# A two-layer graph network on one core: the first pass's weight product, from seven products of halves to fifteen products of thirds

## The chip, the cores and the metric

The kernel runs on one core of one Trainium2 chip. The metric is the device time of one launch in microseconds. Three runs before the change gave 2593.05, 2593.22 and 2594.38 us, a median of 2593.22 us. The profiled execution spans 2591.5 us, and all times of day below count from its start. The engines are named as in the profile: PE is the tensor engine's matmul stream, PEld its weight loads, DVE the vector engine, ACT the scalar engine, POOL GpSimd, SP the engine that issues the DMAs.

## The reference, cut to what matters

The input is x, 128 graphs of 64 nodes with 768 features, and an integer adjacency per graph. Two layers follow each other, each on the normalised and rectified x. The first one is where the change is:

```
h   = relu(layernorm(x))
ctx = adj @ (h @ Wadj.T) / deg + adj.T @ (h @ Wrev.T) / rdeg + h @ Wself.T + biases
x   = x + ctx + (relation counts) @ (embedding tables)
```

Since `adj @ (h @ W) = (adj @ h) @ W`, the kernel mixes the nodes first and multiplies by the weights afterwards. For every pair of 128-row tiles (four graphs, 256 rows), the three terms of ctx together are one product: 256 rows by (3 matrices x 768) inner elements by 768 columns, all in float32. The relation terms are small bfloat16 products of counts with a table, added to the same sums. The second layer is a graph attention with six heads and a gate; its two weight products are of the same kind with two matrices.

## The kernel before

**Two passes.** 8192 rows are 64 tiles of 128 rows, worked on as 32 pairs. The first pass does layer one for all pairs and writes h and x+h of layer two to DRAM; the second pass reads them back and does layer two. Each pass is a loop over pairs.

**The weight product in halves.** In `main(p)` of the first pass the product is taken as a 2x2x2 product of blocks: rows in two tiles, inner elements in two halves of 384, columns in two halves of 384. It is done with seven block products in place of eight (the Winograd form of Strassen's method). The left sums S1 to S4 are formed per pair: S1 and S3 by DVE straight from PSUM in `operands` (lines 441 and 442), S2 and S4 by POOL in `sum2` and `sum4` (lines 447 and 452). The right sums T1 to T4 are formed once, by DVE, at the start (line 184). A block product is 3 blocks of 128 inner elements times 3 matrices, 9 matmuls of 128x128 weights (line 466, the stationary side is the mixed h) against 128x384 moving elements. Every float32 matmul appears twice in the records, with two weight loads. Four PSUM banks, `pwa` to `pwd`, hold chains of partial sums, and after each product DVE adds the bank to a part of x (line 483). A bank that is continued must have been read by DVE before the next product writes it.

**Side work.** While pair p is multiplied, pair p+1 is prepared: load of x and adjacency, normalisation (`norm`, `stats`), mixing with the nodes (`operands`: 24 matmuls of 64 rows and 192 columns, line 422, copied from PSUM by ACT), and relation counts (`count`, `digits`, `count_t`). `finish(p)` normalises the result of pair p for layer two and stores it; its POOL part is a power of one element per row (line 166) and the sum x+h (line 526).

**What sets the order.** `merged(main, side)` interleaves the steps of `main` with entries of a side list, each with the number of the main step it comes before. A scheduler then orders every engine's queue within what dependences allow, apart from instructions marked `keep_in_program_order`. [...] Tiles come from pools with a fixed number of buffers; where a tile has no free buffer, its first writer waits for the last reader of an old one.

**Memory between the passes.** Blocks of weights lie in tiles of their own. The last pair of the first pass fetches the second pass's weights in `fetch` as blocks come free, and forms its T sums. x and the second pass's h share a ring of eight tiles (`bufs=8`, lines 194 and 236). The second pass's head sums `hs` and their swapped halves `hx` share a ring of seven.

Of the kernel before, what the change touches and what calls it, by code (L numbers as in the profile page):

```python
# [15 lines left out]
P = 128  # L16
EPS = 1e-5
NEG_MASK = -999.0
LEAKY = 0.2


@with_exitstack
def kernel(
# [47 lines left out]

    nc = tc.nc
# [11 lines left out]
    HALF = D // 2  # L84
    HH = H // 2
# [9 lines left out]
    assert GT == 2 and N == 64 and DO == P and H == KB and KB % 2 == 0 and H % 2 == 0  # L95
# [76 lines left out]
    def block(name, mats, place):  # L172
        return [keep.tile([P, KH, HALF], F32, name=f"{name}{s}", tag=f"w{place}{s}") if s < 2 else
                keep.tile([P, KH, HALF], F32, name=f"{name}{s}", tag="wl", bufs=7)
                for s in range(mats)]


    SUMS = {"T1": ("T3", "11"), "T2": ("22", "T1"), "T4": ("21", "T2"), "T3": ("22", "T3")}

    def sum_of_weights(w, to, behind=False):  # L180

        a, b = SUMS[to]
        for s, t in enumerate(w[to]):
            ins = nc.vector.tensor_sub(t, w[a][s], w[b][s])  # L184
            if behind:
                tc.keep_in_program_order(ins)


    bv, H1 = {}, {}

    def load_h(p):
        for k in range(2):
            t = 2 * p + k
            H1[t] = keep.tile([P, D], F32, name="h1", tag="x", bufs=8)
            nc.sync.dma_start(H1[t], H1D[p][k * P : (k + 1) * P, :])

    def fetch():

        def blk_of(name, place, h, q):
            bv[name] = block(f"bv{name}", 2, place)  # L200
            for s, src in enumerate((w_cat, hw_t)):
                nc.sync.dma_start(
                    bv[name][s],
                    src[h * HALF : (h + 1) * HALF, q * HALF : (q + 1) * HALF].rearrange(
                        "(k p) n -> p k n", p=P))

        def own(name, place):
            bv[name] = block(f"bv{name}", 2, place)

        return [(4, lambda: load_h(0)),  # L210
                (9, lambda: blk_of("11", "11", 0, 0)),
                (19, lambda: blk_of("21", "21", 1, 0)),
                (28, lambda: blk_of("T3", "T1", 0, 1)),
                (37, lambda: blk_of("22", "T2", 1, 1)),
                (47, lambda: (own("T1", "T4"), sum_of_weights(bv, "T1"), sum_of_weights(bv, "T3"))),
                (58, lambda: (own("T2", "T3"), sum_of_weights(bv, "T2")))]


    with ExitStack() as px:
# [7 lines left out]
        def load(p):  # L227
# [7 lines left out]
            for t in (2 * p, 2 * p + 1):  # L235
                X[t] = keep.tile([P, D], F32, name="x", bufs=8)
                nc.sync.dma_start(X[t], xf[t * P : (t + 1) * P, :])

        load(0)
# [3 lines left out]
        bia = work.tile([5, D], F32, name="bia", tag="s3")  # L243
        for i, v in enumerate((br, brr, badj, brev, bself)):
            nc.scalar.dma_start(bia[i : i + 1, :], row(v, 1))


        bw = {n: block(f"bw{n}", 3, n) for n in ("11", "21", "22", "T1", "T2", "T3", "T4")}

        def load_block(to, h, q):  # L250
            for s, src in enumerate((wadj_t, wrev_t, wself_t)):
                nc.sync.dma_start(
                    to[s], src.rearrange("(k h p) n -> h p k n", h=2, p=P)[h][:, :, q * HALF : (q + 1) * HALF])

        load_block(bw["11"], 0, 0)
        load(1)
        load_block(bw["21"], 1, 0)
        load_block(bw["T3"], 0, 1)
        load_block(bw["22"], 1, 1)
        wrt = work.tile([P, 2, D], F32, name="wrt", tag="a1")  # L260
        nc.sync.dma_start(wrt[:, 0, :], wr_t)
        nc.sync.dma_start(wrt[:, 1, :], wrr_t)
# [22 lines left out]
        def build_table():  # L285
# [21 lines left out]
            for hf in range(2):  # L307
                s = slice(hf * HALF, (hf + 1) * HALF)
                for d in range(2):
                    nc.tensor.matmul(pt[:NROW, hf, :HALF], es[:, d, :], wrt[:, d, s],  # L310
                                     start=(d == 0), stop=False)
                nc.tensor.matmul(pt[:NROW, hf, :HALF], eb, bia[:, s], start=False, stop=True)
            v = work.tile([P, D], F32, name="tv", tag="eq", bufs=1)
            qs = work.tile([P, 3, D], BF16, name="tq", tag="a22")
            nc.scalar.copy(v[:NROW].rearrange("p (a b) -> p a b", a=2), pt[:NROW, :, :HALF])
            for i in range(3):
                q = qs[:, i]
# [7 lines left out]
        A1, A22, S1, S2, S3, S4 = {}, {}, {}, {}, {}, {}  # L325
# [87 lines left out]
        def operands(p, k, q):  # L413
# [12 lines left out]
            pv = ps[:, :, : 6 * N].rearrange("p g (x n) -> p g x n", n=N)  # L426

            def blocks(ap):
                return ap.rearrange("p s (g n) -> p g s n", g=GT)

            if k == 0:
                if q == 0:
                    A1[p] = work.tile([P, KH, 2, 3, P], F32, name="a1")
                nc.scalar.copy(A1[p][:, q].rearrange("p h s (g n) -> p g (h s) n", g=GT), pv)  # L434
                return
            if q == 0:
                A22[p] = work.tile([P, KH, 3, P], F32, name="a22")
                S1[p] = work.tile([P, KH, 3, P], F32, name="s1", bufs=1)
                S3[p] = work.tile([P, KH, 3, P], F32, name="s3")
            nc.scalar.copy(blocks(A22[p][:, q]), pv[:, :, 3:])  # L440
            nc.vector.tensor_sub(blocks(S3[p][:, q]), blocks(A1[p][:, q, 0]), pv[:, :, :3])
            nc.vector.tensor_add(blocks(S1[p][:, q]), blocks(A22[p][:, q]), pv[:, :, :3])

        def sum2(p):
            S2[p] = work.tile([P, KH, 3, P], F32, name="s2", bufs=1)
            for q in range(KH):
                nc.gpsimd.tensor_sub(S2[p][:, q], S1[p][:, q], A1[p][:, q, 0])  # L447

        def sum4(p):
            S4[p] = work.tile([P, KH, 3, P], F32, name="s4", bufs=1)  # L450
            for q in range(KH):
                nc.gpsimd.tensor_sub(S4[p][:, q], A1[p][:, q, 1], S2[p][:, q])

        def main(p):

            bank = {}
            x0, x1 = X[2 * p], X[2 * p + 1]
            steps = []

            def mm(b, a, w, first):  # L460
                for q in range(KH):
                    for s in range(3):
                        def step(q=q, s=s):
                            if first and q == s == 0:
                                bank[b] = psw.tile([P, 512], F32, name=f"pw{b}")
                            nc.tensor.matmul(bank[b][:, :HALF], a()[:, q, s, :], bw[w][s][:, q, :],  # L466
                                             start=(first and q == s == 0),
                                             stop=(q == KH - 1 and s == 2),
                                             skip_group_check=True)
                        steps.append(step)  # L470

            def counts(b, k, q):
                def step():
                    for i, (a, e) in enumerate(PARTS):
                        nc.tensor.matmul(bank[b][:, :HALF], CT_T[p, k][: 3 * (e - a), i, :],  # L475
                                         tabs[i][:, q * HALF : (q + 1) * HALF],
                                         start=False, stop=True, skip_group_check=True)
                steps.append(step)

            def add(xt, q, b):  # L480
                def step():
                    v = xt[:, q * HALF : (q + 1) * HALF]
                    nc.vector.tensor_add(v, bank[b][:, :HALF], v)  # L483
                last = steps[-1]
                steps[-1] = lambda: (last(), step())

            mm("a", lambda: A1[p][:, :, 0], "11", True)
            add(x0, 0, "a")
            mm("c", lambda: A1[p][:, :, 1], "21", True)
            if p:  # L490
                counts("c", 0, 0)
                add(x0, 0, "c")
            mm("b", lambda: S1[p], "T1", True)
            add(x1, 1, "b")
            mm("a", lambda: S2[p], "T2", False)
            add(x0, 1, "a")
            mm("d", lambda: A22[p], "T4", True)
            if p:
                counts("d", 1, 0)
                add(x1, 0, "d")  # L500
            mm("a", lambda: S3[p], "T3", False)
            add(x1, 0, "a")
            mm("b", lambda: S4[p], "22", False)
            n = len(steps)
            counts("a", 1, 1)
            add(x1, 1, "a")
            if p:
                steps.insert(n - 4, steps.pop())
            else:
                counts("c", 0, 0)  # L510
                add(x0, 0, "c")
                counts("d", 1, 0)
                add(x1, 0, "d")
            counts("b", 0, 1)
            add(x0, 1, "b")
# [13 lines left out]
        def side(p):  # L529

            if p >= NP:
                return []
            return [(4, lambda: load(p + 1)),
# [3 lines left out]
                    (6, lambda: prep_r(p)),  # L537
                    (10, lambda: count(p, 0)),
                    (18, lambda: operands(p, 0, 0)),
# [424 lines left out]
```

## Time and profile before

| what | value |
|---|---|
| median time | 2593.22 us |
| PE busy / share of the span | 2543.7 us / 98% |
| weight loads (PEld) busy | 1525.5 us / 59% |
| DVE busy | 1765.7 us / 68% |
| ACT busy | 856.6 us / 33% |
| POOL busy | 733.4 us / 28% |
| one pair of the first pass, by the start of the same chain in neighbouring pairs | 47.36 us |
| first pass ends, first transpose of the second pass | 1554.2 us |
| granted PE clock | 0.994 of full speed |

A busy share is an average over the whole span. To judge a change in one stage, one looks at the period of that stage's loop and at what is idle or waits in it. Rows of the groups have the form: line, engine, operation, out<-in, shapes, count, then busy time in us, the mean of one in ns, and the idle time of the engine just before them with what ended it. Matmul records overlap in the pipeline, so the mean of one (490 ns) is longer than the distance from start to start.

### The profile page before, as it was taken

How to read it: one execution, taken by the hardware profiler on the slowest of the kernel's cores; microseconds unless marked ns; L12 is line 12 of the kernel's file. 1: busy time of each engine (PE TensorE's matmuls, PEld its weight loads, DVE VectorE, ACT ScalarE, POOL GpSimd, SP SyncE). 2: the span in 40 equal slices, each digit the busy share in tenths (PEclk: the TensorE clock that was granted, in tenths of full speed). 3: DMA queues.
4: the chain of work that ended last, by engine and by line, in shares of the span. 5: the costliest groups of instructions: out<-in, count | busy, mean ns of one | idle time of the engine just before them, and what ended most of it. 6: DMA issues, size and time to landing. Idle time of an engine off the chain costs nothing.

```text
span 2591.5 us, 31957 instructions
## 1 busy us (share of the span) xinstructions
PE 2543.7 (98%) x10924; PEld 1525.5 (59%) x10924; DVE 1765.7 (68%) x3887; ACT 856.6 (33%) x2596; POOL 733.4 (28%) x1055
## 2 busy tenths in 40 slices
PE   6999999999999999999999999999999999999996
PEld 3556666556566565565665655656566565565654
DVE  7856566565564665655655435888888888888888
ACT  1111112111111121111111104555555555555555
POOL 2331232232222312322223114333333333333332
PEclk9999999999999999999999999999999999999998
DMA  5112121121121111211211133333333333333322
GB/s 182 44 48 69 39 74 43 39 78 39 39 78 39 61 56 39 78 39 39 78 39 44 67 116 97 106 105 108 105 105 106 103 100 101 100 100 101 100 87 80
DMA packets 101572, 198.78 MB, mean 77 GB/s; under 512 B 35114, under 2 KB 43677, under 8 KB 101410
## 3 DMA queue, kind: packets, MB, share of 16 engines
q1 hardware_dynamic: 101256, 196.70, 23.9%
q8 instruction: 86, 1.41, 0.2%
q14 instruction: 76, 0.62, 0.1%
q10 hardware_dynamic: 154, 0.06, 0.0%
HBM read 95.67 MB, written 75.50 MB: 66 GB/s over the span
## 4 chain that ended last, share of the span: by engine, by line
PE 94%; DVE 3%; DMA 1%; ACT 1%; issue 1%; POOL 0%; SPq 0%; DVEq 0%; ACTq 0%; POOLq 0%
PE pwa L466 21%; PE pwb L466 14%; PE pma L675 14%; PE pmb L675 10%; PE pmc L675 9%; PE pwd L466 7%; PE pwc L466 7%; PE pb L422 5%; PE ps L835 2%; PE ps L646 2%; PE ps L819 1%; PE pwc L475 0%; DMA bw<-in_wadj_t_dram 0%; DVE bwT L184 0%; DMA x<-in_x_dram 0%
## 5 line engine op out<-in xcount | busy, mean ns | idle before, releaser
L466 PE MATMUL pwa<-bwT,s 128*128 128x384 f32 x1152 | 392.5, 490 | 0.4 <-DVE x L483 0.4
L466 PEld LDWEIGHTS pwa<-bwT,s 128*128 128x128 f32 x1152 | 215.5, 190 | 145.9 <-issue 8.0
L675 PE MATMUL pma<-bvT,s 128*128 128x384 f32 x768 | 279.4, 486 | 0.0
L447 POOL TENSOR_TENSOR s<-s,a 128x384 f32<-128x384 f32 x96 | 95.5, 1021 | 644.2 <-PE pwa L466 597.1
L483 DVE TENSOR_TENSOR x<-pwa,x 128x384 f32<-128x384 f32 x128 | 69.5, 543 | 206.8 <-PE pwa L466 170.7
L753 POOL TENSOR_TENSOR pr<-th,wsd 128x768 f32<-128x768 f32 x64 | 119.5, 1867 | 299.8 <-ACT th L751 236.6
L434 ACT COPY a<-pb 128x768 f32<-128x768 f32 x96 | 73.7, 801 | 392.3 <-PE pb L422 392.3
L466 PE MATMUL pwb<-bw,s 128*128 128x384 f32 x576 | 201.5, 489 | 0.0
L466 PE MATMUL pwb<-bwT,s 128*128 128x384 f32 x576 | 199.0, 491 | 0.0
L466 PE MATMUL pwa<-bw,a 128*128 128x384 f32 x576 | 196.2, 489 | 0.0
L466 PE MATMUL pwc<-bw,a 128*128 128x384 f32 x576 | 191.3, 486 | 0.0
L466 PE MATMUL pwd<-bwT,a 128*128 128x384 f32 x576 | 191.3, 486 | 0.0
L411 ACT COPY cntT<-pb 117x128 bf16<-117x128 bf16 (+1 forms) x128 | 27.8, 269 | 484.4 <-PE pb L409 484.4
L675 PEld LDWEIGHTS pma<-bvT,s 128*128 128x128 f32 x768 | 140.0, 190 | 80.8 <-DVE z L701 0.2
L422 PE MATMUL pb<-r,h 64*128 64x192 f32 x1536 | 153.8, 339 | 13.2 <-ACT h L331 6.7
L422 PEld LDWEIGHTS pb<-r,h 64*128 64x128 f32 x1536 | 124.5, 189 | 71.0 <-issue 52.9
L466 PEld LDWEIGHTS pwc<-bw,a 128*128 128x128 f32 x576 | 109.4, 190 | 76.6 <-issue 0.6
L466 PEld LDWEIGHTS pwd<-bwT,a 128*128 128x128 f32 x576 | 109.4, 190 | 76.3 <-issue 0.2
L675 PE MATMUL pmb<-bv,s 128*128 128x384 f32 x384 | 150.7, 502 | 0.0
L466 PEld LDWEIGHTS pwa<-bw,a 128*128 128x128 f32 x576 | 106.7, 191 | 69.4 <-issue 8.4
L466 PEld LDWEIGHTS pwb<-bwT,s 128*128 128x128 f32 x576 | 106.1, 190 | 69.1 <-issue 6.7
L675 PE MATMUL pmb<-bvT,s 128*128 128x384 f32 x384 | 144.3, 486 | 0.0
(155 smaller groups left out, 4723.1 us busy)
## 6 DMA issues: line engine op xcount, KB each, us to landing
x<-in_x_dram SPq DMA_DIRECT2D x64, 384.0 KB
h<-hf SPq DMA_DIRECT2D x64, 384.0 KB
xh<-x SPq DMA_DIRECT2D x64, 384.0 KB
h<-h SPq DMA_DIRECT2D x64, 384.0 KB
x<-xh SPq DMA_DIRECT2D x64, 384.0 KB
hx<-hs SPq DMA_DIRECT2D x128, 192.0 KB
out_dram<-f SPq DMA_DIRECT2D x62, 384.0 KB
ai<-in_adj_dram SPq DMA_DIRECT2D x64, 64.0 KB
```

The costliest lines, as they stand in the source:

```text
L411: nc.scalar.copy(cn[: 3 * (b - a), i, :], pn[: 3 * (b - a), i, :])
L422: nc.tensor.matmul(ps[:, g, i * 3 * N : (i + 1) * 3 * N], H0[t][s, kb * P : (kb + 1) * P], rts[p % 2][s, k].rearrange("p s n -> p (s n)"), ...
L434: nc.scalar.copy(A1[p][:, q].rearrange("p h s (g n) -> p g (h s) n", g=GT), pv)
L447: nc.gpsimd.tensor_sub(S2[p][:, q], S1[p][:, q], A1[p][:, q, 0])
L466: nc.tensor.matmul(bank[b][:, :HALF], a()[:, q, s, :], bw[w][s][:, q, :], start=(first and q == s == 0), stop=(q == KH - 1 and s == 2), sk ...
L483: nc.vector.tensor_add(v, bank[b][:, :HALF], v)
L646: nc.tensor.transpose(ps[:, i, :], H1[2 * p + k][:, kb * P : (kb + 1) * P], ident)
L675: nc.tensor.matmul(bank[b, s][:, :HALF], a[p][:, q, :], bv[w][s][:, q, :], start=(first and q == 0), stop=(q == KH - 1), skip_group_check= ...
L753: nc.gpsimd.tensor_mul(pr, th, wsd[:, 0, :].rearrange("p (h o) -> p h o", h=H))
L819: nc.tensor.transpose(ps[:, c, :], PB[t][:, 2 * c : 2 * c + 2, :].rearrange("p h n -> p (h n)"), ident)
L835: nc.tensor.matmul(po[r][o, c, :], PT[t][s, c, o], (HS if r == g else HX)[t][s, 2 * c + r, :], start=True, stop=True)
```

## The change

The first pass's product is cut as 2 x 3 x 3 instead: rows in two tiles, inner elements in three thirds of 256, columns in three thirds of 256. Such a product has 18 block products; a known scheme does it in 15, at the price of more sums: 11 sums of left blocks per pair (`A_SUMS`) and 13 sums of right blocks once (`B_SUMS`). A block product is now 2 blocks of inner elements x 3 matrices, 6 matmuls against 128x256 moving elements. The purpose is fewer multiplied columns per pair.

What goes with it:

- `PRODUCTS` lists the 15 products in order with bank, sign and the part of x they are added to or subtracted from. Most neighbours in one bank's chain have two other products between them.
- The left operands, blocks and sums alike, are tiles of 128x768 in a ring of 17 (`op`), apart from one block (`oq`). All sums are formed by DVE, in `form`; POOL's S2 and S4 are gone. `operands` only copies, with ACT.
- The six thirds of x of a pair get 15 additions or subtractions of 128x256 and one more for the counts of the part "12".
- The right blocks and sums lie in one region, `weights`, with 15 places of 128x1536. The second pass's weights, its T sums, and its `hs`, `hx` and `hbb` tiles lie in the same region at fixed places.
- The ring of x and h has six tiles instead of eight.
- T4 of the second pass is formed in the last pair of the first pass.

```diff
+PRODUCTS = (
+    ("f1", "g6", "a", True, "11", "+", False),
+    ("f7", "g10", "b", True, "00", "-", False),
+    ("a01", "b11", "d", True, "01", "+", True),
+    ("f4", "b21", "a", False, "01", "-", False),
+    ("a00", "g12", "b", False, "01", "-", False),
+    ("f3", "g8", "c", True, "12", "-", False),
+    ("a02", "g14", "a", False, "00", "-", False),
+    ("f9", "g9", "b", False, "02", "+", False),
+    ("f11", "b10", "d", True, "00", "+", True),
+    ("f6", "g5", "a", False, "02", "+", False),
+    ("f8", "g3", "b", False, "12", "-", False),
+    ("f10", "b12", "c", False, "02", "+", True),
+    ("f5", "b22", "a", False, "12", "-", False),
+    ("a11", "g1", "b", False, "11", "+", True),
+    ("f2", "g11", "a", False, "10", "+", True),
+)
...
+    weights = keep.tile([P, len(PLACES) * PL], F32, name="weights")
...
+    def signed(to, s0, x, s1, y):
+
+        if s0 == "-":
+            return nc.vector.scalar_tensor_tensor(to, x, -1.0, y, op0=OP.mult,
+                                                  op1=OP.add if s1 == "+" else OP.subtract)
+        return (nc.vector.tensor_add if s1 == "+" else nc.vector.tensor_sub)(to, x, y)
...
-            H1[t] = keep.tile([P, D], F32, name="h1", tag="x", bufs=8)
+            H1[t] = keep.tile([P, D], F32, name="h1", tag="x", bufs=6)
...
+        return [(30, lambda: load_h(0)),
+                (13, lambda: blk_of("11", 0, 0)),
+                (20, lambda: blk_of("21", 1, 0)),
+                (31, lambda: blk_of("T3", 0, 1)),
+                (37, lambda: blk_of("22", 1, 1)),
+                (52, lambda: (sum_of_weights("T1"), sum_of_weights("T3"))),
+                (57, lambda: sum_of_weights("T2")),
+                (68, lambda: sum_of_weights("T4"))]
...
-            nc.scalar.copy(blocks(A22[p][:, q]), pv[:, :, 3:])
-            nc.vector.tensor_sub(blocks(S3[p][:, q]), blocks(A1[p][:, q, 0]), pv[:, :, :3])
-            nc.vector.tensor_add(blocks(S1[p][:, q]), blocks(A22[p][:, q]), pv[:, :, :3])
...
+            a = OPS[p, f"a{k}{q}"] = (
+                work.tile([P, KQ, 3, P], F32, name="oq") if (k, q) == (1, 1) else
+                work.tile([P, KQ, 3, P], F32, name="op", bufs=17))
+            nc.scalar.copy(a.rearrange("p h s (g n) -> p g (h s) n", g=GT),
+                           ps[:, :, : 6 * N].rearrange("p g (x n) -> p g x n", n=N))
+
+        def form(p, *names):
+
+            for n in names:
+                s0, x, s1, y = A_SUMS[n]
+                t = OPS[p, n] = work.tile([P, KQ, 3, P], F32, name="op", bufs=17)
+                signed(t, s0, OPS[p, x], s1, OPS[p, y])
...
+            def product(an, bn, b, first, c, sign, cnt):
+                def step(q, s):
+                    if first and q == s == 0:
+                        new(b)
+                    nc.tensor.matmul(
+                        bank[b][:, :CQ], OPS[p, an][:, q, s, :],
+                        bw[bn][:, (s * KQ + q) * CQ : (s * KQ + q + 1) * CQ],
+                        start=(first and q == s == 0), stop=(q == KQ - 1 and s == 2),
+                        skip_group_check=True)
+                    if q == KQ - 1 and s == 2:
+                        if cnt and p:
+                            counts(b, c)
+                        add(b, c, sign)
...
+        for n in ("a12", "a11", "f1", "a00", "a02", "g10", "g6", "f7", "f4", "a10", "a01", "g12", "u",
+                  "g14", "g5", "w", "g8", "f8", "f9", "f2", "f5", "f6", "f3", "g3", "g9", "f10", "f11",
+                  "v", "g1", "g11"):
...
+                        HS[t] = rest[t % 4].rearrange("p (h o) -> p h o", h=H)
```

## The prediction

> **What bounds the kernel now.** I read the engines' shares first, then the chain that ended last:
>
> ```profile
> span 2591.5 us, 31957 instructions
> ...
> PE 2543.7 (98%) x10924; PEld 1525.5 (59%) x10924; DVE 1765.7 (68%) x3887; ACT 856.6 (33%) x2596; POOL 733.4 (28%) x1055
> ...
> PE 94%; DVE 3%; DMA 1%; ACT 1%; issue 1%; POOL 0%; SPq 0%; DVEq 0%; ACTq 0%; POOLq 0%
> ```
>
> The chain lies on PE for 94%. Busy PE is no proof of a full PE, so I took two windows, one in each pass (columns: length, busy time of PE, PEld, DVE, ACT, POOL with counts, clock, DMA):
>
> ```profile
> 802.00:849.00 47.00, 47.00 (x187) 28.18 (x186) 27.55 (x60) 8.29 (x14) 12.06 (x14) 1.00 0.16 54
> 1838.00:1870.00 32.00, 32.00 (x156) 19.18 (x155) 27.03 (x62) 18.47 (x68) 10.49 (x19) 1.00 0.34 104
> ```
>
> PE has no gap in either; DVE works 27.55 of 47 us in the first pass. The chain in order of time gives the first pass's period, and PE's timeline what is in it (start, length, what):
>
> ```profile
> 789.54 5.81 PE pwa L466 x18
> 836.89 5.81 PE pwa L466 x18
> ```
>
> ```profile
> 813.75 1.57 PE L422 MATMUL pb<-r,h 64*128 64x192 f32 x16
> 815.25 0.50 PE L475 MATMUL pwc<-tab,cntT 126*128 126x384 bf16 x2
> ...
> 830.60 5.97 PE L466 MATMUL pwd<-bwT,a 128*128 128x384 f32 x18
> 836.40 0.49 PE L475 MATMUL pwd<-tab,cntT 126*128 126x384 bf16 x2
> 836.73 5.97 PE L466 MATMUL pwa<-bwT,s 128*128 128x384 f32 x18
> ```
>
> A pair takes 836.89 - 789.54 = 47.35, over several pairs 47.36 us. Eighteen records take 836.40 - 830.60 = 5.80 us, so 0.3222 us from start to start at 384 columns; two count records take 0.33 us. What decides is the same number at 256 columns. Shorter matmuls and the weight loads bracket it:
>
> ```profile
> 1813.20 0.49 PE L646 MATMUL ps<-ident,h 128*128 128x128 f32 x3
> 1813.53 0.81 PE L675 MATMUL pma<-bv,a 128*128 128x384 f32 x2
> ```
>
> ```profile
> L422 PEld LDWEIGHTS pb<-r,h 64*128 64x128 f32 x1536 | 124.5, 189 | 71.0 <-issue 52.9 <-ACT h L331 10.9 <-DVE r L373 3.3
> L466 PEld LDWEIGHTS pwd<-bwT,a 128*128 128x128 f32 x576 | 109.4, 190 | 76.3 <-issue 0.2
> L441 DVE TENSOR_TENSOR s<-a,pb 128x384 f32<-128x384 f32 x96 | 52.7, 549 | 96.6 <-ACT a L440 96.6
> L849 DVE SCALAR_TENSOR_TENSOR f<-e,f 128x768 f32<-128x768 f32 x62 | 59.2, 955 | 0.1
> L850 DVE SCALAR_TENSOR_TENSOR f<-f,h 128x768 f32<-128x768 f32 x62 | 107.2, 1730 | 0.0
> L483 DVE TENSOR_TENSOR x<-pwd,x 128x384 f32<-128x384 f32 x32 | 17.8, 557 | 161.7 <-PE pwd L475 161.7
> L370 DVE TENSOR_SCALAR rd<-pb 128x256 f32<-128x256 f32 x32 | 13.1, 410 | 0.2
> ```
>
> Three records of 128 columns take 0.33 us. A weight load lasts 190 ns. The DVE rows price the sums and the additions; line 483 waits for PE, so DVE has time to spare now.
>
> [...]
>
> **The change part by part.**
>
> *Weight product.* Before, 7 x 9 matmuls are 126 records x 0.3222 = 40.60 us. After, 15 x 6 matmuls are 180 records. [...] In line 422's alternating half-array matmuls 16 records take 1.50 us, so each half of the array repeats after 188 ns[...]. At 256 columns 215.5 exceeds 190, by 25 ns. I take 215.5: 38.79 us. Gain 1.81 us per pair.
>
> *Rest of PE.* 47.36 - 40.60 = 6.76 us: mixing, counts, transposes. Counts go from 8 records of 384 (0.163 each, 1.30) to 12 of 256 [...]; mixing keeps 48 records in three groups. So 6.76 stays and a pair takes 45.55 us if PE never waits.
>
> *DVE.* Removed: six sums of line 441/442 (3.2 us) and eight additions (4.4). Added: 11 sums x 0.955 = 10.5 and 16 additions of 256, by line 370's 0.410, 6.6. That is 27.55 - 7.6 + 17.1 = 37.0 us of 45.6, 81%. POOL loses 6 x 1.02 us, which nobody waits for.
>
> *The wait at the pair's end.* Here the queues' order matters. In most places a bank's next product begins two products, 5.2 us, after its last one ended. But the last chain, f2 on bank a, is followed only by a count, one step of f7 and then f1 on bank a. In DVE's queue, between the addition of bank c (f10) and that of f2, stand (in the changed kernel's order of instructions) f9, f2, f5, a subtraction, f6, f3, a statistic, f10, an addition, f11, small statistics, and a value that waits for POOL's power. From start to start a 768 sum takes 0.87 us in the second pass's timeline (line 849 at 1843.04, the next instruction at 1843.91), additions 0.35. Sum: 7 x 0.87 + 4 x 0.35 + 0.85 for statistics + 0.7 for POOL's power (0.56) with its signals + 0.15 for the value = 9.2. PE needs 3 x 2.59 + four count pairs x 0.22 + one step 0.43 = 9.1, with its switches 9.3. A tie: lower bound 0, upper bound 1.83 (POOL's x+h sum, line 526, standing before the power). I take 0.2: 45.75 us.
>
> *Start.* [...] Following the queue from x of pair 1 (about 19 us), bank b's first subtraction stands behind the last right sum, near 55 us, and PE waits for it. I get pair 1 beginning near 94.5 against 89.9 now, and pair 2 near 142 against 139.1: +2.7, between -3 and +12.
>
> *Last pair and second pass.* The T sums stand in DVE's queue among the last pair's additions, before the second-pass weights (4.7 MB, from 16 us on behind freed places) can all have landed: estimate 2 us of PE wait, between 0 and 8. In the second pass the six-tile ring makes the load of h for two pairs ahead wait for line 850 of the previous pair. That ends at 1845.07; the load issued at 1845.10 is complete at 1848.2 by the trace's completion events, and the transpose that needs it is at 1849.50. It fits by 1 us: cost 0. Fixed places for hs and hx: 0, for they come free a pair earlier.
>
> *Sum.* 29 x (47.36 - 45.75) = 46.7, last pair 1.8, less 2.7 and 2: gain 43.8. 2593.2 - 43.8 = 2549 us.
>
> **The rivals.**
>
> *A. DVE is late at every pair's end.* For: the tie above, [...]DVE at 81%. Against: POOL is idle there by my reading, and DVE catches up mid-pair. With 1.2 us of stall instead of 0.2, 30 x 1.0 more: 2579 us.
>
> *B. The sums on DVE run at line 850's price.* For: 1730 ns in place of 955 for one operation, at times when POOL works. Then the seven sums at the pair's end cost 7 x 0.78 = 5.4 us more, all on the path: 2549 + 30 x 5.4 = 2711, slower than before. Against: POOL's two-tensor work in a pair falls from 9.8 to 3.7 us and lies at the pair's start.
>
> *C. The second pass waits for h.* For: 1 us of margin. If the load lands 3 us later, 2 us x 30: 2609, slower. Against: the second pass keeps its period in the trace, the order of its DVE, ACT and POOL queues is unchanged, and the transfer is the same size at the same time.
>
> *D. All ties fall well.* No stall, start no later: 2549 - 30 x 0.2 - 6 - 2 = 2535.
>
> **How the numbers follow.** The forecast, with small errors of each term, 0.62; D 0.10; A 0.17; B 0.05; C 0.06. The predicted time is the forecast's, 2549. Low: D's 2535 less 3 for the start, 2532. High: A with 1.3 us and a late start, 2584. Slower than 2593 by over 0.2%: B and C, 0.11. Same: the upper tail of A, 0.03. Faster: 0.86.
>
> **What would show each step.** Right: eighteen records' place taken by twelve in 2.59 us; pairs 45.6 to 46 us apart; PE without gaps in mid-pair; line 541's last addition on bank a ending just as the next f1 begins; a second pass of 1037 us. Wrong: records 230 ns or more apart (the load shows); a regular gap before f1 <- DVE (A), or in front of f4 or f9 too; DVE sums of 1.2 us or more (B); gaps before the second pass's transposes ended by a DMA (C); pair 2 beginning after 150 us.

## The result, and the profile after

The changed kernel takes 2554.55 us (median of 4 runs, 2554.14 to 2556.60) against 2593.38 us for the kernel before in the same session (2593.05 to 2594.38). The ratio is 0.9851, with a 95% interval of 0.9834 to 0.9868: faster by 1.5%. The forecast was 2549 us, with 2532 to 2584 as its range. The profiled executions differ by 2591.5 - 2552.4 = 39.1 us; the forecast's gain was 43.8. The runs of one kernel lie 1 to 7 us apart in what follows, and each trace is that of one run.

First the page of the changed kernel: span, shares, and the chain by engine.

```profile
span 2552.4 us, 35949 instructions
...
PE 2501.2 (98%) x12780; PEld 1858.1 (73%) x12780; DVE 1977.2 (77%) x4309; ACT 887.8 (35%) x2596; POOL 566.0 (22%) x863
...
PE 92%; DVE 3%; DMA 2%; issue 1%; POOL 1%; ACT 1%; SPq 0%; DVEq 0%; POOLq 0%; ACTq 0%
```

PE is the bound as before, with more and shorter records; weight loads rise from 59% to 73% of the span, and DVE from 68% to 77%. Next the first pass's window, with columns as in the prediction, and then the chain in order of time and PE's timeline (start, length, what):

```profile
802.00:849.00 47.00, 47.00 (x252) 39.71 (x251) 34.17 (x74) 9.26 (x14) 7.24 (x8) 1.00 0.16 54
```

```profile
784.62 2.71 PE pwa L549 x12
830.57 2.72 PE pwa L549 x12
```

```profile
814.00 2.75 PE L549 MATMUL pwb<-weights,op 128*128 128x256 f32 x12
816.59 1.89 PE L549 MATMUL pwc<-weights,op 128*128 128x256 f32 x8
```

PE still has no gap in the window, with 252 records in place of 187. A pair takes 830.57 - 784.62 = 45.95 us against 47.36. A product's twelve records take 816.59 - 814.00 = 2.59 us, 0.2158 each. Two rows of the groups answer to the prediction's prices:

```profile
L549 PEld LDWEIGHTS pwa<-weights,op 128*128 128x128 f32 x2304 | 423.3, 190 | 73.3 <-DVE x L541 11.7 <-issue 7.0 <-DVE x L543 1.2
L245 DVE TENSOR_TENSOR op<-op 128x768 f32<-128x768 f32 x256 | 238.7, 953 | 154.2 <-ACT op L510 154.1
```

The left sums on DVE cost 953 ns each, and they wait for ACT's copies of the mixed blocks (154 us in all): DVE has time to spare.

**Where the 39.1 us come from**, by the two traces. One matmul per pair, for the degrees (line 448, formerly 368), marks the pairs, which are counted from 0; below, "pair 2 begins at" means the time of this matmul in pair 2. First two times of the kernel before, then the same two of the changed kernel:

```profile
142.81 0.27 PE L368 MATMUL pb<-ab,blkb 128*128 128x256 bf16 x1
1554.24 0.82 PE L646 MATMUL ps<-ident,h 128*128 128x128 f32 x6
```

```profile
144.72 0.27 PE L448 MATMUL pb<-ab,blkb 128*128 128x256 bf16 x1
1513.94 0.82 PE L709 MATMUL ps<-ident,h 128*128 128x128 f32 x6
```

Pair 2 begins 144.72 - 142.81 = 1.9 us later: -1.9. The 28 distances from there to the matmul of pair 30 are shorter by 1.41 us each, but for one of 46.29 us: +39.0. (In that pair an x tile was loaded late: the chain shows a store from the ring of x, 4.58 us long, ahead of the load. No pair of the kernel before stands out like that.) From the last of these matmuls to the first transpose of the second pass it takes 82.26 us against 85.44: +3.2, of which 1.4 belong to pair 30 and 1.8 to the last pair. The second pass is 1.1 us longer: -1.1. The sum is 39.2.

Inside a steady pair, the distances from start to start, summed by line, give:

| us per pair | before | after |
|---|---|---|
| weight product (126 / 180 records) | 41.18 | 39.68 |
| mixing (48) | 4.51 | 4.50 |
| counts (8 / 12) | 1.33 | 1.35 |
| transposes of counts (4) | 0.23 | 0.31 |
| degrees (1) | 0.11 | 0.11 |
| sum | 47.36 | 45.95 |

### The profile page after: what moved, and what is told of

The parts are those of the page before. It is cut to its first block, busy times and chain, and to the rows that moved or that the text cites. A ratio compares the mean times of both kernels' runs of the same rounds, so it can differ in the third digit from the quotient of the medians.

```text
span 2552.4 us, 35949 instructions
## 1 busy us (share of the span) xinstructions
PE 2501.2 (98%) x12780; PEld 1858.1 (73%) x12780; DVE 1977.2 (77%) x4309; ACT 887.8 (35%) x2596; POOL 566.0 (22%) x863
## 4 chain that ended last, share of the span: by engine, by line
PE 92%; DVE 3%; DMA 2%; issue 1%; POOL 1%; ACT 1%; SPq 0%; DVEq 0%; POOLq 0%; ACTq 0%
PE pwa L549 19%; PE pwb L549 16%; PE pma L738 14%; PE pmb L738 10%; PE pmc L738 9%; PE pwc L549 6%; PE pwd L549 6%; PE pb L502 5%; PE ps L898 2%; PE ps L709 2%; PE ps L882 1%; PE pwd L533 1%; DVE op L245 1%; DVE weights L245 0%; DMA weights<-in_wself_t_dram 0%
## 5 line engine op out<-in xcount | busy, mean ns | idle before, releaser
L549 PE MATMUL pwa<-weights,op 128*128 128x256 f32 x2304 | 542.8, 383 | 4.1 <-DVE x L541 2.9
L549 PEld LDWEIGHTS pwa<-weights,op 128*128 128x128 f32 x2304 | 423.3, 190 | 73.3 <-DVE x L541 11.7
L549 PE MATMUL pwb<-weights,op 128*128 128x256 f32 x1536 | 372.5, 383 | 12.6 <-DVE x L543 9.5
L245 DVE TENSOR_TENSOR op<-op 128x768 f32<-128x768 f32 x256 | 238.7, 953 | 154.2 <-ACT op L510 154.1
L549 PEld LDWEIGHTS pwb<-weights,op 128*128 128x128 f32 x1536 | 285.8, 191 | 60.8 <-DVE x L543 10.7
L738 PE MATMUL pmb<-weights,s 128*128 128x384 f32 x768 | 295.1, 494 | 0.5 <-DVE s L723 0.5
L738 PE MATMUL pmc<-weights,a 128*128 128x384 f32 x768 | 285.4, 488 | 0.0
L738 PE MATMUL pma<-weights,s 128*128 128x384 f32 x768 | 279.4, 486 | 0.0
L738 PEld LDWEIGHTS pmc<-weights,a 128*128 128x128 f32 x768 | 136.5, 190 | 81.9 <-issue 12.3
L816 POOL TENSOR_TENSOR pr<-th,wsd 128x768 f32<-128x768 f32 x64 | 119.5, 1868 | 299.6 <-ACT th L814 236.4
L549 PE MATMUL pwc<-weights,op 128*128 128x256 f32 x768 | 184.9, 383 | 0.0
L549 PE MATMUL pwd<-weights,op 128*128 128x256 f32 x768 | 176.2, 379 | 0.0
```

What stands on the lines that cost most here:

```text
L245: return (nc.vector.tensor_add if s1 == "+" else nc.vector.tensor_sub)(to, x, y)
L549: nc.tensor.matmul(bank[b][:, :CQ], OPS[p, an][:, q, s, :], bw[bn][:, (s * KQ + q) * CQ : (s * KQ + q + 1) * CQ], start=(first and q == s ...
L738: nc.tensor.matmul(bank[b, s][:, :HALF], a[p][:, q, :], bv[w][s][:, q, :], start=(first and q == 0), stop=(q == KH - 1), skip_group_check= ...
L816: nc.gpsimd.tensor_mul(pr, th, wsd[:, 0, :].rearrange("p (h o) -> p h o", h=H))
```

## The experiments

The nine runs below stand on the changed kernel. The kernel before took 2593.2 to 2593.5 us (medians) beside them. A product is named by its left operand: f1, on bank a, is the first one of a pair, f7 on bank b the second, and f2 on bank a the last. Each expectation names a theory and a rival, and the text says which of them the run bears out.

**One sum more at the pair's end.** The prediction took DVE's chain there to be as long as PE's.

```diff
-            return [(0, lambda: form(p, "f5", "f6", "f3")),
+            return [(0, lambda: form(p, "f5", "f6", "f3")),
+                    (0, lambda: again(p, "f3")),
```

> Edit to the changed kernel (2554.5 us): the left sum f3 is written twice in each pair but the first, the second time with the same result, so that DVE has one sum of 0.87 to 0.95 us more between the last additions of two pairs. Theory (tie, DVE's chain at the pair's end is as long as PE's): each pair gets longer by nearly all of it, 0.7 to 0.95 us, 31 pairs: 2576 to 2584 us, with a gap on PE before f1, ended by DVE's addition on bank a. Rival (there is slack of a microsecond or more, and the 0.35 us per pair come from PE's own records): 2554 to 2558 us.

It took 2558.05 us (2557.02 to 2559.42), the rival's time, and the steady pair took 45.96 us: the theory of the tie falls. First the changed kernel's timeline at a pair's end, then the same place of this one:

```profile
829.27 0.55 POOL L226 TENSOR_TENSOR rn<-ve,mhalf 128x1 f32<-128x1 f32 x1 [2.29 <-DVE ve L225]
829.52 0.39 PE L533 MATMUL pwa<-tab,cntT 126*128 126x256 bf16 x2
829.75 0.39 PE L533 MATMUL pwd<-tab,cntT 126*128 126x256 bf16 x2
829.85 0.16 DVE L227 SCALAR_TENSOR_TENSOR rn<-mv,rn 128x1 f32<-128x1 f32 x1 [0.73 <-POOL rn L226]
829.95 0.42 DVE L541 TENSOR_TENSOR x<-pwa,x 128x256 f32<-128x256 f32 x1
829.97 0.60 PE L549 MATMUL pwb<-weights,op 128*128 128x256 f32 x2
830.42 1.78 PE L549 MATMUL pwa<-weights,op 128*128 128x256 f32 x7
```

```profile
785.70 0.96 DVE L245 TENSOR_TENSOR op<-op 128x768 f32<-128x768 f32 x1
...
786.13 0.39 PE L533 MATMUL pwa<-tab,cntT 126*128 126x256 bf16 x2
786.57 0.41 DVE L541 TENSOR_TENSOR x<-pwa,x 128x256 f32<-128x256 f32 x1
787.04 2.86 PE L549 MATMUL pwa<-weights,op 128*128 128x256 f32 x12
787.24 0.15 DVE L227 SCALAR_TENSOR_TENSOR rn<-mv,rn 128x1 f32<-128x1 f32 x1
```

The scheduler put the extra sum where DVE had waited 0.73 us for POOL, and moved the value that needs POOL (line 227) behind the addition. DVE's queue reaches the addition just in time in both, so they can't tell alone what releases it: it starts 829.95 - 829.52 = 0.43 us after PE's count on bank a in the first timeline and 0.44 in the second. The last pair of the changed kernel can, for there DVE stands idle ahead of it:

```profile
1513.49 0.39 PE L533 MATMUL pwa<-tab,cntT 126*128 126x256 bf16 x2
1513.91 0.42 DVE L541 TENSOR_TENSOR x<-pwa,x 128x256 f32<-128x256 f32 x1 [2.39 <-PE pwa L533]
```

It is 0.42 us there. So f1's small delay is the way from PE to DVE and back on one bank, and an idle DVE would not have shortened it by more than some 0.02 us. The profiled execution is 3.0 us longer than the changed kernel's, and 2.4 of them lie ahead of pair 2, which begins at 147.13 instead of 144.72.

**Two sums more.** The same with f6 written twice as well.

> Edit to the changed kernel (2554.5 us): two left sums per pair are written twice, f3 and f6, each with the same result. With one sum twice the steady pair took 45.96 us against 45.95: the sum (0.86 us from start to start) filled the time in which DVE had waited for POOL's power, 0.73 us, ahead of bank a's last addition. Theory (after that DVE's chain is as long as PE's to some 0.1 us): the second sum is on the path whole, 0.8 to 0.95 us per pair, 2580 to 2588 us, with a gap on PE before f1 ended by DVE's addition. Rival (DVE's chain still has over 0.8 us to spare, since the planner moves other work behind the addition): 2558 to 2564 us.

It took 2559.06 us (2556.27 to 2563.24), and the steady pair 45.97: the rival. The scheduler moved f11 behind the addition. DVE's order isn't fixed, and the slack is larger than the prediction's fixed order allowed. The profiled execution, of 2563.24 us, lost its time elsewhere: 2.4 us ahead of pair 2, and 5.6 in the second pass. There the first pair, from its first transpose to the next pair's, takes 13.8 us instead of 9.65; what holds it up is not shown.

**Another product first.**

```diff
-    ("f1", "g6", "a", True, "11", "+", False),
     ("f7", "g10", "b", True, "00", "-", False),
+    ("f1", "g6", "a", True, "11", "+", False),
```

> Edit to the changed kernel (2554.5 us): the first two products change places, f7 x g10 on bank b first, then f1 x g6 on bank a. Theory (tie at the pair's end: bank a's last addition ends at 830.37 us and f1 begins at 830.42, one record late by 0.125 us): bank a has 2.6 us more, f1 begins without a wait, 0.12 us per pair less, 30 pairs: 2550 to 2551 us, and the first records of both products stand 0.216 apart. Rival (the late record is the weight load after a mixing or count block, not a wait for DVE): the extra 0.12 stays, 2554 +- 1.

It took 2550.47 us (2549.64 to 2551.12), ratio 0.9834 (0.9819 to 0.9849), and the steady pair 45.83: the theory. PE's timeline at a pair's start, f7 and then f1:

```profile
782.76 2.75 PE L549 MATMUL pwb<-weights,op 128*128 128x256 f32 x12
785.36 1.46 PE L549 MATMUL pwa<-weights,op 128*128 128x256 f32 x6
```

Twelve undisturbed records, 2.60 us, and f1 follows. What the exchange removes are two long distances of the changed kernel: there f1's first record comes 0.236 us after the one before it instead of 0.216, and the next one 0.320 later, together 0.125 too much. The same 0.104 us longer distance follows nearly every mixing block in both kernels (0.427 against 0.322 before). The expectation had called the delay a wait for DVE; by the two runs above it is the round trip on bank a. Of all versions this is the fastest with the whole computation.

**Three right sums later.**

```diff
-                  "v", "g1", "g11"):
+                  ):
...
-        late = [(20, build_table), (22, lambda: count(0, 0)),
+        late = [(34, lambda: form_b("v")), (42, lambda: form_b("g1")), (50, lambda: form_b("g11")),
+                (20, build_table), (22, lambda: count(0, 0)),
```

> Edit to the changed kernel (2554.5 us): the last three right sums (v, g1, g11), needed only by the 14th and 15th product, leave the list ahead of the loop and go among pair 0's steps. Theory (DVE's queue sets the start: the first subtraction of bank b at 52.85 us stands behind two weight sums and a reciprocal, and PE waits 8.7 us for it): most of that wait goes; the three sums take 3 x 1.7 us out of its way, so 2548 to 2551 us, and the first passes' later pairs stay at 45.95. Rival (the weights' transfers, or PE's own work, set the start): the wait moves to another releaser, 2554 +- 1.

It took 2557.37 us (2556.71 to 2558.59), slower than both the theory and the rival foretold, by little more than the runs of one kernel differ. In the changed kernel PE's timeline shows the wait that the edit aims at:

```profile
53.28 5.47 PE L549 MATMUL pwb<-weights,op 128*128 128x256 f32 x12 [8.71 <-DVE x L543]
```

It went, and pair 1's degree matmul came at 89.63 instead of 94.72. But then the chain in order of time, in this kernel, shows:

```profile
104.16 2.49 DVE op L245
...
108.45 0.34 DVE x L543
108.83 5.49 PE pwa L549 x12
```

PE waited 5.87 us ahead of 108.83 for a subtraction behind a reduction of 1.8 us and a left sum of 2.5 us, which ran beside POOL's x+h sum (1.80 us from 104.04). Pair 2 began at 147.41, 2.7 us later than without the edit. DVE's busy time from 20 to 147 us is 119.5 us here and 119.7 in the changed kernel, 94% of the window: the work was moved, not lessened. The windows up to pair 2, with columns as in the prediction, show what that did to PE, first in the changed kernel, then in this one:

```profile
0.00:144.72 144.72, 114.52 (x573) 91.55 (x574) 131.73 (x263) 29.33 (x43) 20.05 (x37) 0.95 0.31 99
0.00:147.41 147.41, 116.61 (x574) 92.47 (x575) 134.51 (x263) 29.60 (x44) 19.94 (x37) 0.95 0.30 97
```

PE stood idle for 147.41 - 116.61 = 30.8 us, against 30.2 in the changed kernel. The other 2.1 us are the same records running longer. Where that comes from is seen in this window of the changed kernel, right after its wait of 8.71 us:

```profile
53.20:58.60 5.40, 5.32 (x13) 4.25 (x14) 5.40 (x10) 0.00 (x0) 0.00 (x0) 0.50 0.00 0
```

The granted clock was 0.50, and the twelve records took 58.56 - 53.28 = 5.28 us instead of 2.59. The twelve records at 108.83 in this run took 5.28 us too.

**Both edits.**

> Both edits to the changed kernel (2554.5 us): three right sums among pair 0's steps, and f7 x g10 ahead of f1 x g6. Alone the first gave 2557.4 (pair 1 began 5 us earlier, and pair 2 2.7 us later, for PE waited 6.2 us at 108.8 for a subtraction of bank a behind a 2.57 us sum beside POOL's work), and the second 2550.5. Theory (DVE's work in the first 150 us is what counts, and deferring moves it only): 2550 to 2554 us. Rival (with another product first the late subtraction is no longer in the way, and the 5 us stay): 2545 to 2547 us.

It took 2554.89 us (2552.03 to 2556.61), 0.9 us beyond the theory's upper end; steady pairs take 45.83 us, and pair 2 begins at 147.94. With the exchange alone it begins at 142.74. PE stands idle for as long up to there in both (28.9 and 28.8 us), but the same records take 119.0 us instead of 114.0, at a mean granted clock of 0.93 instead of 0.95. The trace is of the run of 2556.61 us; whether the edit brings the lower clock in every run is not shown. The rival, in which the 5 us stay, falls.

**No right sums.**

```diff
-            tc.keep_in_program_order(signed(bw[n], s0, bw[x], s1, bw[y]))
+            bw[n] = bw[x]
```

> The changed kernel without its 13 right sums: each product takes the first operand of its right sum in place of the sum, so the weight product is of other numbers; the left sums, transfers, products and additions stay. Theory (DVE's work sets the start: deferring three sums only moved the wait, while leaving out 13 x 1.67 = 21.7 us of DVE work takes it away): PE's 9.1 us wait at 53.3 and the smaller ones near 22 to 39 and 102 to 141 us mostly go, pair 2 begins 10 to 17 us earlier, steady pairs stay at 45.95: 2537 to 2545 us. Rival (PE waits in the start for the weights' transfers or for POOL and ACT, and DVE would be late anyway): 2550 to 2556 us.

It took 2536.64 us (2536.29 to 2538.94), 17.9 us less than the changed kernel: the theory, 0.4 us beyond its lower end. Steady pairs stay at 45.95, and pair 2 begins at 127.32 instead of 144.72. First the window up to there in this run, then one of the changed kernel:

```profile
0.00:127.32 127.32, 109.43 (x574) 88.62 (x574) 110.82 (x250) 29.31 (x44) 19.93 (x37) 1.00 0.41 134
```

```profile
20.00:53.00 33.00, 19.89 (x73) 13.87 (x73) 33.00 (x30) 3.58 (x5) 0.55 (x1) 0.88 0.46 146
```

Leaving out 21.7 us of sums takes 12.3 us off PE's idle time (17.9 instead of 30.2), and 5.1 off the time that the same records take, at a clock of 1.00 instead of 0.95. The edit also spares the products some weight blocks that they no longer read. But in the changed kernel DVE is busy for all of the 33 us from 20 to 53, so no transfer and no other engine held it up there. With the deferral this settles the start: it is the amount of DVE's work that sets it; the one other order tried did not help.

**Fewer columns.** How near was the weight load, 190 ns, to being the pace?

```diff
+                    n = CQ if first and q == s == 0 else 192
...
-                        bw[bn][:, (s * KQ + q) * CQ : (s * KQ + q + 1) * CQ],
+                        bw[bn][:, (s * KQ + q) * CQ : (s * KQ + q) * CQ + n],
```

> The changed kernel with 192 of 256 columns in all matmuls of the weight product but the first of each bank (the last 64 columns of each block product are left out). Theory (a record lasts as long as the longer of its two streamings,[...] and its weight load, 190 ns): records stand 0.188 to 0.191 us apart, twelve in 2.27, and a pair falls from 45.95 to about 41.4 us, 2554.5 - 30 x 4.6 = 2417 us, or somewhat more where DVE becomes late. Rival (the streamings alone set the pace): 0.162 us, twelve in 1.95, with PE waiting for DVE between the products.

It took 2290.30 us (2289.49 to 2292.02), and a pair 36.98: the rival's pace, without the waits between products that it had added. PE's timeline of this kernel, and its row of weight loads:

```profile
704.27 2.11 PE L550 MATMUL pwa<-weights,op 128*128 128x192 f32 x12
706.22 1.46 PE L550 MATMUL pwb<-weights,op 128*128 128x192 f32 x8
```

```profile
L550 PEld LDWEIGHTS pwa<-weights,op 128*128 128x128 f32 x2304 | 375.8, 191 | 21.4 <-issue 7.0
```

Twelve records take 706.22 - 704.27 = 1.95 us, 0.1625 each, near the changed kernel's 0.2158 scaled by the columns (0.1619). A load still lasts 191 ns, and PE has no gap: the loads overlap each other, 2304 of them in 375.8 us of busy time where their lengths add up to 440. So the length of a load's record, 191 ns, is not its pace here. (The theory's "two streamings" agree with the kernel before: at 384 columns a float32 record stands 0.322 us from the next one, a bfloat16 count record 0.163.) No trace here shows full-array float32 records closer than 0.11 us, the 128-column transposes that the prediction quotes, whose loads last 141 ns; at what distance the load would set the pace is not shown. In this run DVE works 42.3 us of a 47 us window in the first pass, and PE has no gap in it.

**Two left sums on POOL.**

```diff
+                if p and n in ("f6", "f3"):
+                    (nc.gpsimd.tensor_sub if s1 == "-" else nc.gpsimd.tensor_add)(
+                        t, OPS[p, x], OPS[p, y])
+                    continue
```

> Edit to the changed kernel (2554.5 us): the left sums f3 and f6 go to POOL (not in pair 0), where one takes 1.0 us by the row of the x + h sum; DVE has two sums of 0.95 us less per pair. Theory (the tie costs only 0.12 us per pair now): DVE's chain shortens by 1.7 us, f1 no longer waits, 2550 to 2551 us. Rival (DVE's sums beside POOL's two-tensor work take 1.73 us instead of 0.95, the prediction's rival B): f5, f2, f10 or f11 take up to 0.78 us more each, the gain at the tie is lost again, 2554 to 2575 us, and the mean of the 128x768 sums on DVE rises above 1.0 us.

It took 2585.46 us (2582.37 to 2588.57), 31 us more than the changed kernel: the rival, and beyond its upper end. (The 1.0 us expected for POOL's sum was that of a 384-column one; x+h at 768 takes 1.81.) The timeline at a pair's end (the last line is f1), and DVE's row of sums:

```profile
748.79 4.29 POOL L519 TENSOR_TENSOR op<-op 128x768 f32<-128x768 f32 x2 [18.45 <-DVE op L243]
749.34 2.08 DVE L245 TENSOR_TENSOR op<-op 128x768 f32<-128x768 f32 x1
751.52 2.38 DVE L245 TENSOR_TENSOR op<-op 128x768 f32<-128x768 f32 x1
...
755.57 1.78 PE L553 MATMUL pwa<-weights,op 128*128 128x256 f32 x7 [0.52 <-DVE x L545]
```

```profile
L245 DVE TENSOR_TENSOR op<-op 128x768 f32<-128x768 f32 x194 | 259.3, 1349 | 152.5 <-ACT op L510 152.5
```

While POOL spends 4.29 us on two sums, DVE's own two take 2.08 and 2.38 us; alone they take some 1.9 together. They stand ahead of bank a's addition, and now f1 does wait for DVE, 0.52 us in the line above. The pair takes 46.80 us, 0.85 more. Of the 34.4 us that the profiled execution is longer, 5.6 lie ahead of pair 2 (150.30) and 3.8 in the second pass; the rest are the pairs. Beside POOL's sums DVE's 953 ns became 2.08 and 2.38 us, and the mean of the row rose to 1349 ns.

**Plain products.** Thirds, ring and region kept, but 18 block products without sums. In the last pair some of the second pass's weights arrive in their places before the product has used the old ones, so that pair's product is of other numbers.

```diff
+PRODUCTS = tuple(
+    (f"a{k}{j}", f"b{j}{q}", "abcd"[(3 * k + q) % 4], j == 0, f"{k}{q}", "+" if j == 2 else "",
+     j == 2 and (k, q) != (1, 2))
+    for k, q in ((0, 0), (0, 1), (0, 2), (1, 0), (1, 1), (1, 2)) for j in range(3)
+)
```

> The changed kernel with thirds, ring and the one region for weights kept, but the weight product in the plain 18 block products, three to an output's bank and one addition each, without left or right sums. Theory (the gain comes from the number of streamed columns alone: 36 more records of 0.2158 us): 7.77 us more per pair, less the 0.12 us before f1 and some switches, 53.3 to 53.8 us per pair, and a start that is 5 to 15 us earlier without the 13 right sums: 2765 to 2790 us. Rival (DVE's and the banks' waits cost the changed kernel more than the trace shows, and plain products win some of it back): pairs under 53 us, below 2760.

It took 2783.18 us (2782.82 to 2784.46), a pair 53.60: the theory. Against the changed kernel it is 7.65 us more per pair, with 36 x 0.2158 = 7.77 expected for the records, less the 0.125 at f1. Pair 2 begins at 143.42, 1.3 us earlier, though pairs 0 and 1 have 15.3 us more to multiply: without sums the start is some 16.6 us shorter, a little more than was expected and near the run above without right sums. DVE falls to 57% of the span and nothing is won by it. So the gain of the change is the number of streamed columns; the sums that buy it are hidden in the steady pairs, and paid at the start.

## Why the prediction was right, and where it was off

- **Weight product.** Right: 2.59 us for twelve records, 0.2158 against 0.2155 foretold; 180 x 0.2158 = 38.84 against 38.79. The 0.2155 was the author's estimate; the trace of before gives 0.2148, if its 0.3222 at 384 columns is scaled to 256. The argument for the weight load was wrong in one point. It read "215.5 exceeds 190, by 25 ns" as the margin, though its own line of 128-column transposes, 0.11 us apart under loads of 141 ns, spoke against that; at 192 columns records stand 162.5 ns apart under loads of 191. The margin was larger than believed, so the number held. What paces line 422's half-array records was not tried.
- **Rest of PE.** Too low by a little: "6.76 stays". The table's counts and transposes add 0.10 us. Beyond 126 x 0.3222 = 40.60, the product's own distances had an excess of 0.58 us before; beyond 38.84 they have 0.84 now: one more edge of a mixing block falls inside a product (0.1), the count transposes disturb two records instead of one (0.05), and f1's 0.125 is in it.
- **DVE.** 37.0 us foretold, 34.2 in the window of 47 us (about 33.4 per pair). The prediction added the lengths of records, 0.955 and 0.410 us, where the next one begins after 0.87 and some 0.34: about 2 us of the difference. The sums' price held (953 ns, 0.87 from start to start), and rival B's price did not appear in steady pairs.
- **The pair's end.** "A tie", with 0.2 us of stall: the size was near (0.125), the cause wrong. The count itself came out: from bank c's addition to the end of bank a's DVE takes 830.37 - 821.31 = 9.06 us, 9.2 foretold. But it was taken for a fixed order, and 0.73 us of waiting for POOL for work; one and two more sums cost 0.01 and 0.02 us per pair. The exchange of two products removes the 0.125. Rival A falls with it.
- **Start.** +2.7 foretold, +1.9 measured. The reason given was right: bank b's first subtraction stands behind the last right sums (52.85 us, foretold "near 55"). One takes 1755 ns, 1.67 us from start to start, all thirteen 21.7 us; leaving them out takes 17.4 us away. The way there was not, and part of the near sum is luck: pair 1 was to begin 4.6 us later than before, and by its degree matmul it begins 1.0 later (94.72 against 93.75). The rest was lost within pair 1, whose waits come to 2.8 us against 1.4. That records run at a granted clock of 0.50 after the wait of 8.71 us was not looked for.
- **Last pair.** "2 us of PE wait" for the T sums: none. The last pair gained 1.8, the 1.8 of the forecast without its wait, instead of losing 0.2.
- **The range.** Rival D takes 6 us off for a start that is "no later", where only 2.7 had been put on, and the low end takes another 3 off for the start. By its own terms it lies some 3 us too low; nothing hung on it.
- **Second pass.** "It fits by 1 us: cost 0" held for the ring: the period is 31.65 us in both kernels, and rival C falls. But the pass is 1.1 us longer, 0.7 of it in its first pair: from its first transpose to that of the next pair it takes 9.65 us instead of 8.98, and 9.65 to 9.73 in six of the runs above. (The other 0.5 stand in the last pair, whose length varies from 81.9 to 83.9 us over these runs.) In the first pair the changed kernel's timeline shows:

```profile
1517.09 0.32 POOL L698 MEMSET lrow<- 32x64 bf16 x2
1518.39 0.55 POOL L226 TENSOR_TENSOR rn<-ve,mhalf 128x1 f32<-128x1 f32 x1
1518.98 0.16 DVE L227 SCALAR_TENSOR_TENSOR rn<-mv,rn 128x1 f32<-128x1 f32 x1 [2.95 <-POOL rn L226]
1520.26 2.20 PE L738 MATMUL pmb<-weights,s 128*128 128x384 f32 x6 [0.52 <-DVE s L723]
```

POOL fills the second pass's constants ahead of the power that finishes the last pair; DVE waits 2.95 us for it, with the operand of PE's third product behind it in the queue. In the kernel before, that operand was formed ahead of the value. The prediction did not look there. This is read from the traces and was not tried alone.

The step that missed most is the sum's first term: 46.7 became 40.5 (29 pairs, 40.8, less 0.3 for the one with a late tile), for a pair gained 1.41 us instead of 1.61 (0.05 of the record's size, 0.10 of transposes and counts, 0.26 of the product's excess, less the 0.2 foretold as stall). The last pair gave 2.0 of it back, the start 0.8, and the second pass took 1.1. So the total lies nearer to the forecast than its largest term does, because errors of both signs met.

## What to carry to other kernels

Price a change of tiling by the distance from start to start at the new size, then add what each interruption of the stream costs; here the columns gave 1.76 us per pair and the interruptions took 0.35 back. A fixed number of sums made once is not free because the loop hides its own: at the start nothing hid them (17.4 us here), and shifting three of them did not help while that engine was full (94% of the window here). Look at the clock beside the waits: 5.1 of the 17.4 us that the right sums cost were records at a lower clock, not waiting. Before a queue is counted instruction by instruction to a tie, put one more instruction in: a scheduler may have room that the count doesn't show.

## What the runs showed that was not expected

- After waits of 8.71 and 5.87 us on PE, the next twelve records took 5.28 us instead of 2.59; the granted clock was 0.50 in the window after the first of them.
- At 192 columns weight loads of 191 ns follow each other every 162.5 ns, without a gap on PE.
- The record after an interruption of the stream stands 0.10 us further off, in both kernels and at both sizes (0.427 against 0.322, 0.320 against 0.216). What causes it is not shown.
- DVE and POOL together, on two-operand sums from SBUF, did not do more than DVE alone in the run with two left sums on POOL: four sums, and some 0.7 us of statistics on DVE, in about 5.1 us (748.79 to 753.90), where DVE alone takes 3.8 for the sums by its 953 ns.
